# A two-layer gated transformer on one core: the opening of layer 1 reordered

## The chip, the cores and the metric

One core of a Trainium2 chip runs the whole computation in one launch. The core has these engines: PE (TensorE, matrix products), DVE (VectorE), ACT (ScalarE), POOL (GpSimd) and SP, whose queue issues nearly all transfers between the chip's memory (DRAM) and the on-chip memory; POOL has a queue for transfers of its own. Every queue works strictly in the order in which the program put its instructions. The metric is the device time of one execution in microseconds (us), median of several runs.

## The reference, cut to what matters

Eight sequences (elements) x of 512 tokens by 256 channels pass through two layers, each an attention part and a feed-forward part (ffn), each part added through a gate. Cut to the order of the parts:

```python
x = x + tanh(g_xattn[0]) * L0_xattn(layernorm(x), ctx)     # self + cross attention, 16 heads of 16
x = x + tanh(g_ffn[0])   * L0_ffn(layernorm(x))            # 8-bit quantised, scales over ALL elements
x = x + tanh(g_xattn[1]) * L1_xattn(layernorm(x), ctx)     # two blocks a1, a2 with an mlp each
x = x + tanh(g_ffn[1])   * L1_ffn(layernorm(x))            # ternary weights, conv of width 3
```

Two things matter for what follows. The second matrix product of L0_ffn takes h = gelu(...) quantised by a scale and a zero point that come from the minimum and maximum of h over all eight elements: it can't begin before the last h is known. And block a2 of L1_xattn attends from x to the normalised context, whose keys and values don't depend on x at all:

```python
yn = ln(ee)                       # ee: the context, 512 tokens by 128 channels
k = einsum('btc,hcd->bhtd', yn, wk); v = einsum('btc,hcd->bhtd', yn, wv)   # "second" keys and values
```

In layer 1, x first goes through two normalisations in a row (that of the layer and ln1; the kernel makes them in one step), then one more inside block a1; then come queries, keys and values, 16 heads of 32, the scores and their exponentials, the weighted sum, and the mlp (li1, li2, gelu, li3).

## The kernel before, in words

**Stages.** `layer0_xattn` keeps all eight x on chip. In its sixth and seventh turn `load1` (line 1460) loads the projection weights of layer 1, folds gains and biases into them, and keeps them: those of block a2 other than wq lie in a pool (`w8`) that ends with layer 0. `ctx0` writes the normalised, transposed context of each element to DRAM (`cd`). `layer0_ffn` (line 1525) makes h of each element (`range0`), writes it to DRAM (`hd`) and takes its extrema (line 1621); beside that, `keys2` (line 1629) makes the second keys and values of each element from `cd` (eight projections of 128x128 by 128x512 each), writes them to `kd` and `vd`. After the last extremum, scales are computed (line 1546 on), all tiles of layer 0 are given up, and `layer1_xattn` (line 1661) begins.

**Opening of layer 1.** `first(b)` (line 1807) completes layer 0 for element b, in two halves of 256 tokens: load a half of h (tile `hF`, one buffer), quantise on ACT (line 1828), clamp and cast to `hq` on DVE (lines 1830 and 1832, one buffer), multiply by w2 (tile `fw`) on PE, add to x (`xF`, line 1839), store that half of x to `xd` (line 1802). `pre1(b, half)` (line 1882) then loads the half back (tile `xP`, line 1798), normalises it for the layer and ln1 in one step (`ln_timed`, lines 1843 to 1862: statistics on DVE, a power on POOL, a scaling on ACT or DVE), adds rows (lines 1912 and 1914), normalises it again for block a1, stores the residual to `rd` (line 1918), turns it on PE into `zT`, and makes the values. `pair1` makes queries and keys of a group of four heads, `steps1` has the scores (`ps_s`), the exponentials (tile `pt`, three buffers, `PTS`), and the weighted sums. `load_mlp` loads li1, li2 and li3 of block a1 (2.5 MB, line 1770), `mlp1` (line 1969) uses them.

**The planner.** The order of all instructions is written out by a planner when the program is built. `Pace` (line 744) keeps an estimated clock per engine and per tile; transfers are planned one behind the other on one wire at 280 bytes per ns. Work is cut into streams, which are generators that say at each `yield` what they need next. `weave_all` (line 1713) holds chains of streams: `few` (the `first` of the elements, `load_mlp`, and `last`, the ffn of layer 1, sorted by base), `pairs`, two of `mlps`, two of `pres`, `diag`, beside the attention steps. Only the head of a chain can go on. At each point it takes, among the candidates that could start within 0.3 us of PE's planned time, the one of lowest `base + share * done / total`, where done is PE work planned so far; attention step n of the k-th of 16 slots has k + n/16. If none can start, it takes the one that can start soonest. The slots run element 0 block a1, element 1 block a1, element 0 block a2, element 1 block a2, and so on in pairs of elements. Each engine then runs in exactly that order, whatever the real times are.

**Lines that the change touches.** The streams of the opening are made here:

```python
for k, b in zip((-1, 0, 1, 2, 3, 4, 7, 8), range(B)):
    few.append(Stream(self.first(b), 3.8, 0.8, k))
    if not b:
        few.append(Stream(self.load_mlp(), 1.0, 1.0, k))
```

Of the kernel before, what the change touches and what calls it, by code (L numbers as in the profile page):

```python
# [15 lines left out]
P = 128  # L16
# [10 lines left out]
NEG = -1.0e30  # L27
PTS = 3


# [901 lines left out]
class Fast(General):  # L932
# [8 lines left out]
    def setup(self, ctx, ctx0):  # L941
        super().setup(ctx, ctx0)
        nc, tc = self.nc, self.tc
        dram = ctx.enter_context(tc.tile_pool(name="dram", bufs=1, space=bass.MemoryType.DRAM))

        def scratch(name, shape, dtype=F32):
            return [dram.tile(shape, dtype, name=f"{name}{b}") for b in range(B)]


        self.xd = [scratch(f"xd{k}_", [P, NT * C]) for k in range(3)]  # L950

        self.rd = scratch("rd", [P, NT * C])
        self.hd = scratch("hd", [P, NF * T])
        self.cd = scratch("cd", [P, T])
        self.kd = scratch("kd", [P, 4 * T])
        self.vd = scratch("vd", [P, NT * 2 * C])
        self.fwd = {
            n: dram.tile([P, 2 * FF], BF16, name=f"q_{n}")
            for n in ("f0_w1", "f0_w2", "f1_w1", "f1_w2")
        }  # L960
        keep = self.keep2
        self.ones = keep.tile([P, 32], F32, name="ones")
        nc.vector.memset(self.ones, 1.0)

# [495 lines left out]
    def load1(self, blk):  # L1460
# [13 lines left out]
        for name, nch, ln in (("wq", 2, "lnx"), ("wk", nchy, "lny"), ("wv", nchy, "lny")):  # L1474
# [14 lines left out]
            else:  # L1489
                for g in range(4):  # L1490
                    for c in range(nch):
# [3 lines left out]
                        )  # L1495
                bias = home.tile([P, 4], F32, name=f"{pre}_{name}_b")
                s = 32.0 ** -0.5 if name == "wq" else 1.0
# [6 lines left out]
        self.w1s.append(w)  # L1504
        if blk:

            a, e = at["li1"]
# [17 lines left out]
    def layer0_ffn(self):  # L1525
        nc, tc, small = self.nc, self.tc, self.small
        with (
# [101 lines left out]
    def keys2(self, b):  # L1629

        nc, work, w = self.nc, self.work, self.w1s[1]
        cT = self.cTs.pop(0)
        if b + 2 < B:
# [7 lines left out]
        v = work.tile([P, NT, 2 * C], F32, tag="v2", name="v2")  # L1641
        for kt in range(NT):
            yield need(cT)
            ps = self.bank()
            self.mm(ps, cT[:, 0, kt * P : (kt + 1) * P], w["wv"][:, 0, :])
            self.copy_of(v[:, kt, :], ps)
        nc.sync.dma_start(self.vd[b], v.rearrange("p t c -> p (t c)"))

# [12 lines left out]
    def layer1_xattn(self):  # L1661
        nc, tc = self.nc, self.tc
        with (
# [143 lines left out]
    def first(self, b):  # L1807
# [4 lines left out]
        def load_h(half):  # L1812
            h = work.tile([P, NF, n], F32, tag="hF", name="hF")
            nc.sync.dma_start(
                h, self.hd[b].rearrange("p (f t) -> p f t", f=NF)[:, :, half * n : (half + 1) * n]
            )
            return h

        h = load_h(0)
        w2, = self.few_weights(0, ("w2",))  # L1820
        x = self.load_x(0, b, "xF")
        yield need(x, pe=False)
        nc.gpsimd.tensor_tensor(x, x, self.gb2.unsqueeze(1).to_broadcast([P, NT, C]), ALU.add)
        for half in range(2):
            if half:
                h = load_h(1)
            yield need(h, pe=False)
# [11 lines left out]
            nc.vector.scalar_tensor_tensor(x2, ps, self.sg, x2, ALU.mult, ALU.add)  # L1839
            self.store_x(1, b, x2, half)  # L1840
            self.given.add((1, b, half))

# [39 lines left out]
    def pre1(self, b, half):  # L1882
# [86 lines left out]
    def mlp1(self, b, blk, half):  # L1969
# [3 lines left out]
        pre = ("a1", "a2")[blk]  # L1973
        while self.both_in.get((b, blk), 0) < 2:
            yield WAIT
# [488 lines left out]
```

## Time and profile before

| | us |
|---|---|
| median of 3 runs | 2920.08 |
| lowest and highest | 2911.39, 2924.05 |
| the profiled execution | 2911.77 |
| its span, first to last instruction | 2910.0 |
| PE busy | 2551.4 (88%) |
| DVE busy | 1707.2 (59%) |
| ACT busy | 1496.4 (51%) |
| POOL busy | 628.6 (22%) |
| DRAM traffic | 116.32 MB read, 62.39 MB written |

The page of the profile gives busy time by engine, the span in 40 slices of 72.75 us (a digit is the busy share in tenths), the transfer queues, and the costliest groups of instructions by line. The other views are: a table of busy time by stretch, the timeline of one engine (start, length, engine, line, operation, tiles written and read, and in brackets how long the engine stood idle before and what ended it), and who waited for whom. SPq is SP's queue: the length of its entries is the issue, not the transfer. Layer 0's attention ends near 770 us, its ffn at 911.7, and the attention of layer 1 runs from 980.7.

### The profile page before, as it was taken

How to read it: one execution, taken by the hardware profiler on the slowest of the kernel's cores; microseconds unless marked ns; L12 is line 12 of the kernel's file. 1: busy time of each engine (PE TensorE's matmuls, PEld its weight loads, DVE VectorE, ACT ScalarE, POOL GpSimd, SP SyncE). 2: the span in 40 equal slices, each digit the busy share in tenths (PEclk: the TensorE clock that was granted, in tenths of full speed). 3: DMA queues.
4: the chain of work that ended last, by engine and by line, in shares of the span. 5: the costliest groups of instructions: out<-in, count | busy, mean ns of one | idle time of the engine just before them, and what ended most of it. 6: DMA issues, size and time to landing. Idle time of an engine off the chain costs nothing. (4 is left out here: it accounts for less than half of the span.)

```text
span 2910.0 us, 38485 instructions
## 1 busy us (share of the span) xinstructions
PE 2551.4 (88%) x15431; PEld 1234.3 (42%) x15436; DVE 1707.2 (59%) x2998; ACT 1496.4 (51%) x1852; POOL 628.6 (22%) x691
## 2 busy tenths in 40 slices
PE   5999999999774889999988898998898998898976
PEld 2333333333232335535554534455443555353454
DVE  2434443444375465574657786746878446778574
ACT  2666666656584445555435555444555444455531
POOL 2111121121100343330423202322312122321010
PEclk9999999999997899999999999999999999999987
DMA  3011110100165312222110212220120111021100
GB/s 107 8 41 48 48 40 31 41 15 12 66 280 207 126 63 72 70 91 73 70 51 26 77 48 73 87 98 1 48 90 26 48 43 38 26 94 34 44 15 16
DMA packets 77179, 181.27 MB, mean 62 GB/s; under 512 B 7488, under 2 KB 36544, under 8 KB 69184
## 3 DMA queue, kind: packets, MB, share of 16 engines
q1 hardware_dynamic: 74768, 176.05, 17.4%
q8 instruction: 123, 2.02, 0.3%
q0 software_dynamic: 640, 2.10, 0.3%
q10 hardware_dynamic: 1584, 0.58, 0.1%
q14 instruction: 64, 0.52, 0.1%
HBM read 116.32 MB, written 62.39 MB: 61 GB/s over the span
## 5 line engine op out<-in xcount | busy, mean ns | idle before, releaser
L2084 ACT ACTIVATE pt<-ps_s 128x1024 f32<-128x1024 f32 x512 | 496.0, 1020 | 385.9 <-PE ps_s L1012 327.1
L1012 PE MATMUL ps_s<-QT,KT 32*128 32x512 f32 (+3 forms) x4096 | 634.1, 613 | 59.8 <-DVE KT L1655 26.3
L1371 ACT ACTIVATE pt<-ps_s 128x1024 f32<-128x1024 f32 (+3 forms) x512 | 411.6, 861 | 203.4 <-PE ps_s L1012 197.6
L1012 PEld LDWEIGHTS ps_s<-QT,KT 32*128 32x128 f32 x4096 | 199.3, 186 | 415.9 <-issue 235.3
L1012 PE MATMUL ov<-pt,v 128*32 128x512 f32 (+3 forms) x2048 | 237.9, 535 | 12.9 <-POOL pt L1374 12.5
L1012 PE MATMUL ps<-x3T,li 128*128 128x256 f32 x1024 | 247.3, 395 | 0.2 <-ACT x3T L2001 0.2
L2088 POOL TENSOR_SCALAR_AFFINE_SELECT dg<-pt 128x512 f32<-128x512 f32 x128 | 114.6, 897 | 593.0 <-ACT pt L2084 593.0
L1012 PE MATMUL ps<-li,hD 128*128 128x256 f32 x1024 | 236.3, 384 | 5.3 <-ACT hD L2031 5.3
L1012 PE MATMUL ov<-pt,vt 128*32 128x512 f32 (+3 forms) x1792 | 201.2, 520 | 36.4 <-DVE oT L2133 26.4
L1012 PEld LDWEIGHTS ps<-x3T,li 128*128 128x128 f32 x1024 | 196.5, 197 | 56.4 <-issue 18.0
L1012 PEld LDWEIGHTS ps<-li,hD 128*128 128x128 f32 x1024 | 189.6, 190 | 64.1 <-issue 17.7
L1856 POOL TENSOR_SCALAR mv<-mv 128x2 f32<-128x2 f32 (+1 forms) x105 | 61.9, 589 | 688.7 <-DVE mv L1851 631.5
L1374 POOL TENSOR_SCALAR_AFFINE_SELECT pt<-pt 128x512 f32<-128x512 f32 x128 | 86.8, 678 | 476.0 <-ACT pt L1371 476.0
L2115 DVE TENSOR_TENSOR acc<-acc,pt 128x2048 f32<-128x2048 f32 x64 | 148.6, 2323 | 6.9 <-ACT pt L2084 6.4
L2113 DVE TENSOR_TENSOR acc<-pt 128x2048 f32<-128x2048 f32 x64 | 151.2, 2362 | 1.0 <-ACT pt L2084 1.0
L2199 DVE SCALAR_TENSOR_TENSOR hF<-hp,cols,hF 128x256 f32<-128x256 f32 x224 | 121.9, 544 | 33.9 <-ACT hF L2190 27.4
L1396 DVE STREAM_TRANSPOSE ot<-ov 128x512 f32<-128x512 f32 x64 | 45.8, 716 | 155.8 <-PE ov L1012 155.8
L1012 PE MATMUL ps<-zT,a_wq 128*128 128x512 f32 x256 | 127.9, 623 | 1.4 <-DVE x3T L2003 1.1
L1012 PE MATMUL ps<-li,oT 128*128 128x256 f32 x512 | 126.6, 390 | 2.8 <-DVE oT L2133 2.2
L1012 PE MATMUL ps<-fw,hq 128*128 128x256 bf16 x512 | 72.6, 304 | 62.6 <-DVE hq L1832 44.6
L1015 PE MATMUL ps<-ident,z 128*128 128x128 f32 x328 | 64.5, 318 | 70.9 <-DVE z L136 40.9
L1655 DVE TENSOR_SCALAR hD<-ps,cols 128x256 f32<-128x256 f32 x145 | 66.9, 481 | 98.2 <-PE ps L1012 72.5
(277 smaller groups left out, 3666.2 us busy)
## 6 DMA issues: line engine op xcount, KB each, us to landing
hd<-h SPq DMA_DIRECT2D x16, 1024.0 KB, 3.9
hF<-hd SPq DMA_DIRECT2D x16, 1024.0 KB, 6.3
li<-in_w_a_dram SPq DMA_DIRECT2D x16, 1024.0 KB, 5.1
fw<-q_f_w SPq DMA_DIRECT2D x22, 512.0 KB, 5.8
xF<-xd SPq DMA_DIRECT2D x22, 512.0 KB, 5.3
kd<-k SPq DMA_DIRECT2D x8, 1024.0 KB, 4.0
vd<-v SPq DMA_DIRECT2D x8, 1024.0 KB, 5.5
res<-rd SPq DMA_DIRECT2D x32, 256.0 KB, 2.8
```

The costliest lines, as they stand in the source:

```text
L1012: self.nc.tensor.matmul(out, lhsT, rhs, start=start, stop=stop, skip_group_check=True)
L1015: self.nc.tensor.transpose(out, in_, self.ident)
L1371: nc.scalar.activation(pt[:, 2 * jp : 2 * jp + 2, lo:], pss[jp][:, :, lo:], AF.Exp)
L1374: nc.gpsimd.affine_select(out=diag, in_=diag, compare_op=ALU.is_ge, fill=0.0, base=0, pattern=[[0, 4], [1, P]], channel_multiplier=-1,)
L1396: nc.vector.transpose(ot.rearrange("p b d -> p (b d)"), ov)
L1655: self.nc.vector.tensor_scalar(out, ps, bias, None, ALU.add)
L1856: nc.gpsimd.tensor_scalar(rstd, mv[:, :, 1], EPS, None, ALU.add)
L2084: nc.scalar.activation(pt[:, 2 * jp : 2 * jp + 2, :], pss[jp], AF.Exp)
L2088: nc.gpsimd.affine_select(out=dg, in_=pt[:, :, diag], compare_op=ALU.is_gt, fill=0.0, base=0, pattern=[[0, 4], [-1, P]], channel_multiplier=1,
L2113: nc.vector.tensor_tensor(st["acc"], st["pt"], pt, ALU.add)
L2115: nc.vector.tensor_tensor(st["acc"], st["acc"], pt, ALU.add)
L2199: nc.vector.scalar_tensor_tensor(a, hp[:, half + k : half + k + n], self.col("conv_w", 3 * f + k), a, ALU.mult, ALU.add)
```

## The change

Four things are done.

1. The second keys and values of elements 6 and 7 are no longer made in the ffn of layer 0 but by a new stream `keys2_rest` in layer 1, base -1, share 1 over 16 us of work. Since their weights lie in a pool that has ended by then, `load1` writes them to DRAM (`wd`, two stores of 256 KB on SP), and the new stream loads them and the two contexts through POOL's queue (four loads of 256 KB) into tiles whose buffers the mlp uses later (`xo`, `x3T`); the keys and values themselves go into `pt` buffers, and from there to `kd` and `vd`. `mlp1` waits until all are made (`keys_done`). The bias wk_b now lies in a pool that lasts.
2. `first(0)` loads both halves of h at its start, the second into a `pt` buffer.
3. x of element 0 stays on chip in `xF`: `pre1(0, half)` reads it there in place of loading `xP`; its last normalisation writes into an `xP` tile. The store to `xd` stays, since block a2 reads it later. `first(1)`, whose x goes into the same buffer, waits until both halves have been read (`x0_read`).
4. `load_mlp` comes after `first(1)` in its chain, not after `first(0)`.

```diff
+KEYS_FIRST = 6
...
+        self.wd = [dram.tile([P, 2 * C], F32, name=f"wd{i}") for i in range(2)]
...
-                bias = home.tile([P, 4], F32, name=f"{pre}_{name}_b")
+                bias = self.keep2.tile([P, 4], F32, name=f"{pre}_{name}_b")
...
         if blk:
+            for i, name in enumerate(("wk", "wv")):
+                nc.sync.dma_start(self.wd[i], w[name].rearrange("p c f -> p (c f)"))
...
-            streams.append(Stream(self.chain(*(self.keys2(b) for b in range(B))), 64.0, B))
+            streams.append(Stream(self.chain(*(self.keys2(b) for b in range(KEYS_FIRST))), 64.0, B))
...
+    def keys2_rest(self):
+
+        nc, work = self.nc, self.work
+        w = []
+        for i in range(2):
+            t = work.tile([P, 1, 2 * C], F32, tag=f"xo{i}", name="w2")
+            nc.gpsimd.dma_start(t[:, 0, :], self.wd[i])
+            w.append(t)
+        cTs = {}
+
+        def load(b):
+            if b < B:
+                cTs[b] = work.tile([P, 1, T], F32, tag=f"x3T{b % 2}", name="cT")
+                nc.gpsimd.dma_start(cTs[b][:, 0, :], self.cd[b])
+
+        load(KEYS_FIRST)
+        load(KEYS_FIRST + 1)
+        for b in range(KEYS_FIRST, B):
+            k = work.tile([P, 4, T], F32, tag="pt", name="k2", bufs=PTS)
+            yield from self.keys_of(b, cTs[b], w[0], k)
+            v = work.tile([P, NT, 2 * C], F32, tag="pt", name="v2", bufs=PTS)
+            yield from self.values_of(b, cTs.pop(b), w[1], v)
+            load(b + 2)
+        self.keys_done = True
+
+    def keys_of(self, b, cT, wk, k):
+        bias = self.w1s[1]["wk_b"]
         for g in range(4):
-            yield need(cT)
-            ps = self.proj(w["wk"], cT, g * P)
-            self.plus(k[:, g, :], ps, w["wk_b"][:, g : g + 1])
-        nc.sync.dma_start(self.kd[b], k.rearrange("p g t -> p (g t)"))
+            yield need(cT, wk)
+            ps = self.proj(wk, cT, g * P)
+            self.plus(k[:, g, :], ps, bias[:, g : g + 1])
+        self.nc.sync.dma_start(self.kd[b], k.rearrange("p g t -> p (g t)"))
...
-                if not b:
+                if b == 1:
                     few.append(Stream(self.load_mlp(), 1.0, 1.0, k))
...
+            self.keys_done, self.x0_read = False, 0
+            keys = [Stream(self.keys2_rest(), 8.0 * (B - KEYS_FIRST), 1.0, -1.0)]
             self.weave_all(
-                [self.steps1(b, blk) for b, blk in order], [few, pairs, *mlps, *pres, diag]
+                [self.steps1(b, blk) for b, blk in order], [few, pairs, *mlps, *pres, diag, keys]
             )
...
         def load_h(half):
-            h = work.tile([P, NF, n], F32, tag="hF", name="hF")
+            if b or not half:
+                h = work.tile([P, NF, n], F32, tag="hF", name="hF")
+            else:
+                h = work.tile([P, NF, n], F32, tag="pt", name="hF", bufs=PTS)
...
+        while b == 1 and self.x0_read < 2:
+            yield WAIT
         h = load_h(0)
         w2, = self.few_weights(0, ("w2",))
         x = self.load_x(0, b, "xF")
+        h2 = None if b else load_h(1)
...
-                h = load_h(1)
+                h = h2 or load_h(1)
...
             self.store_x(1, b, x2, half)
+            if not b:
+                self.x0 = x
...
-        x = self.load_x(1, b, f"xP{half}", half)
+        if b:
+            z = x = self.load_x(1, b, f"xP{half}", half)
+        else:
+            x = self.x0[:, 2 * half : 2 * half + 2, :]
+            z = work.tile([P, 2, C], F32, tag=f"xP{half}", name="xP")
         yield need(x, pe=False)
         res = work.tile([P, 2, C], F32, tag=f"resP{half}", name="resP")
         yield from self.ln_timed(x, res, f"p{half}", of_ln=True)
-        yield from self.enter1(b, half, "ln1", "a1", res, x, f"p{half}")
+        self.x0_read += not b
+        yield from self.enter1(b, half, "ln1", "a1", res, z, f"p{half}")
...
-        while self.both_in.get((b, blk), 0) < 2:
+        while self.both_in.get((b, blk), 0) < 2 or not self.keys_done:
             yield WAIT
```

The new function `values_of` is the second half of the former `keys2`, with the weights given as an argument, as `keys_of` is the first.

More of the change, by code (lines that the diff above doesn't have):

```diff
@@ L1629, in keys2 @@
     def keys2(self, b):
-        nc, work, w = self.nc, self.work, self.w1s[1]
+        work, w = self.work, self.w1s[1]
         cT = self.cTs.pop(0)
-        if b + 2 < B:
+        if b + 2 < KEYS_FIRST:
             self.load_cT(b + 2)
         k = work.tile([P, 4, T], F32, tag="k2", name="k2")
-        for g in range(4):
-            yield need(cT)
-            ps = self.proj(w["wk"], cT, g * P)
-            self.plus(k[:, g, :], ps, w["wk_b"][:, g : g + 1])
-        nc.sync.dma_start(self.kd[b], k.rearrange("p g t -> p (g t)"))
@@ L1641, in keys2 @@
-        v = work.tile([P, NT, 2 * C], F32, tag="v2", name="v2")
+        yield from self.keys_of(b, cT, w["wk"], k)
+        v = work.tile([P, NT, 2 * C], F32, tag="v2", name="v2")
+        yield from self.values_of(b, cT, w["wv"], v)
+    def keys2_rest(self):
[19 more added lines that the diff above has]
+        self.keys_done = True
@@ L1642, in keys2, with values_of @@
+    def keys_of(self, b, cT, wk, k):
+        bias = self.w1s[1]["wk_b"]
+        for g in range(4):
+            yield need(cT, wk)
+            ps = self.proj(wk, cT, g * P)
+            self.plus(k[:, g, :], ps, bias[:, g : g + 1])
+        self.nc.sync.dma_start(self.kd[b], k.rearrange("p g t -> p (g t)"))
+    def values_of(self, b, cT, wv, v):
         for kt in range(NT):
-            yield need(cT)
+            yield need(cT, wv)
             ps = self.bank()
-            self.mm(ps, cT[:, 0, kt * P : (kt + 1) * P], w["wv"][:, 0, :])
+            self.mm(ps, cT[:, 0, kt * P : (kt + 1) * P], wv[:, 0, :])
@@ L1646, in keys2 @@
             self.copy_of(v[:, kt, :], ps)
-        nc.sync.dma_start(self.vd[b], v.rearrange("p t c -> p (t c)"))
+        self.nc.sync.dma_start(self.vd[b], v.rearrange("p t c -> p (t c)"))
     def plus(self, out, ps, bias):
```

## The prediction

> **What bounds the kernel now.** I read the page first, for where TensorE (PE) is not busy; then the table of busy time by stretch around that place; then the timeline of every engine there, step by step; last the waits of SP, whose queue feeds nearly all loads.
>
> ```profile
> span 2910.0 us, 38485 instructions
> ...
> PE   5999999999774889999988898998898998898976
> ...
> PEclk9999999999997899999999999999999999999987
> ```
>
> A slice is 72.75 us. PE is busy nearly everywhere except in slices 10 to 12 (727 to 946 us), where the granted clock falls too. That is the end of layer 0 and the opening of layer 1. Columns below: stretch, its length, busy time of PE, weight loads, DVE, ACT, POOL, then clock, DMA share, GB/s.
>
> ```profile
> 912.00:924.00 12.00, 0.25 (x2) 0.22 (x3) 4.31 (x16) 2.09 (x1) 0.86 (x3) 0.50 0.49 176
> ...
> 928.00:939.00 11.00, 0.00 (x0) 0.00 (x0) 3.18 (x6) 2.09 (x1) 1.59 (x2) 0.59 0.45 143
> ...
> 944.00:956.00 12.00, 7.30 (x12) 2.95 (x12) 3.20 (x9) 1.09 (x2) 2.22 (x3) 0.72 0.93 323
> 956.00:971.00 15.00, 5.03 (x21) 3.01 (x21) 8.46 (x14) 4.75 (x6) 8.55 (x7) 0.66 0.29 109
> ...
> 981.00:1053.00 72.00, 63.05 (x484) 23.19 (x476) 44.34 (x53) 40.08 (x42) 28.59 (x28) 0.93 0.19 63
> 1053.00:1069.00 16.00, 12.22 (x32) 5.42 (x28) 10.75 (x22) 3.88 (x7) 4.51 (x5) 0.89 0.05 17
> ```
>
> No engine is full between 912 and 971: this stretch is one chain of small steps and round trips to memory. From the timelines of SP, ACT, DVE and PE (start, length, engine, line; in brackets the engine's idle time before and what ended it):
>
> ```profile
> 912.08 0.62 SPq L1814 DMA_DIRECT2D hF<-hd  x1
> ...
> 918.92 2.09 ACT L1828 ACTIVATE hF<-hF,magic,qh_rs 128x2048 f32<-128x2048 f32 x1 [13.33 <-DMA fw<-q_f_w]
> ...
> 927.09 0.75 DVE L1839 SCALAR_TENSOR_TENSOR xF<-ps,sg,xF 128x512 f32<-128x512 f32 x1 [3.44 <-PE ps L1012]
> ...
> 928.23 0.53 SPq L1814 DMA_DIRECT2D hF<-hd  x1
> ...
> 934.76 2.09 ACT L1828 ACTIVATE hF<-hF,magic,qh_rs 128x2048 f32<-128x2048 f32 x1 [13.75 <-DMA hF<-hd]
> ...
> 943.18 0.75 DVE L1839 SCALAR_TENSOR_TENSOR xF<-ps,sg,xF 128x512 f32<-128x512 f32 x1 [1.76 <-PE ps L1012]
> ...
> 946.37 0.33 SPq L1798 DMA_DIRECT2D xP<-xd  x1
> ...
> 952.85 18.14 SPq L1918 DMA_DIRECT2D rd<-resP  x2
> ...
> 955.90 0.42 DVE L1850 BATCH_NORM_STATS2 mv<-xP 128x6 f32<-128x256 f32 x1
> ...
> 970.28 0.59 ACT L1930 COPY zT<-ps 128x512 f32<-128x512 f32 x1 [0.99 <-PE ps L1015]
> ...
> 980.66 1.14 PE L1012 MATMUL ps_s<-QT,KT 32*128 32x512 f32 x8 [0.94 <-DVE KT L1655]
> ...
> 1069.32 1.14 PE L1012 MATMUL ps_s<-QT,KT 32*128 32x512 f32 x8 [0.78 <-ACT KT L1653]
> ```
>
> See: the second half of h is asked for only when the first is consumed (928.23); the finished x goes out and comes back as xP, arriving 12.0 us after 943.93 because 2.5 MB of mlp weights (issued 944.32) go ahead; scores of element 0 begin at 980.66, those of element 1 at 1069.32, after a thin stretch from 1053.
>
> **The change, part by part.** All against the profiled execution, 2911.77 us (span 2910.0), which is 8.3 below the median 2920.08 and at the low end of the runs shown.
>
> **Layer 0.** Two 256 KB stores join SP after the scaling of a_wk and a_wv (DVE, done 601.8 and 605.8). SP waits there; behind it is the li_b load, which moves from 541.15 to about 606.5 and with its 6.2 us lands at 612.7, just before its matmuls at 613.20; the next SP item, the cd store, comes at 613.03. Cost 0, at worst 2 if that cover slips.
>
> **The ffn of layer 0 loses 16 projections**: PE 16 x 0.86 = 13.8 us, ACT 8 x 0.69 + 8 x 0.59 = 10.2 us. But the loop there is set by DVE: four reductions 8.87, two xq evacuations 1.40, then a gap until ACT has four gelus; the starts of the reductions lie 14.23, 13.51, 13.47, 13.51, 13.47, 14.18, 13.51 apart. Keys fill gaps. The only turn without keys beside its start (807.06 to 821.29) is one of the long ones: PE had stood 9.75 us and its twelve matmuls took 4.86 instead of 2.96. So the last two turns should be 14.2 each: **+0.7** (ends: -5 if the gap closed and DVE's own 11.0 per turn ruled, +1.4).
>
> **Loads at once.** hF behind nothing took 928.23 to 934.76, 6.5; hF with 1 MB behind it in the queue took 912.08 to 918.92, 6.8. So what follows in SP's queue delays it little; with 1 MB of hF and 1 MB from POOL added I take 919.5 (ends: 918.9, and 924 if all 4.2 MB shared 401 GB/s equally). POOL's four issues at 0.54 to 0.98 end by 917; its next work, xF plus bias, began at 924.12: covered. The first half is then done at 919.5 + 8.9 = 928.4 (before: 927.84).
>
> The Trainium skill, page "DMA: Bandwidth & Descriptors", section "Queues, rings and completion order", says that every DMA engine takes turns between the queues that have work, packet by packet, so POOL's megabyte would halve hF's rate. That would cost about 2.6 us (estimate, 1 MB at the trace's 401 GB/s) and make the sum -15 in place of -17.5; no stretch of this trace has both queues loaded at once.
>
> **Second half.** Its data lie there by about 924; only the cast waits, since hq has one buffer, read by PE until 927.6. But the planner decides PE's order: the keys stream has base -1 and rises 1 per 16 us of planned work, first(0) stands at -1 + 0.8 x 0.5 = -0.6 after its first half. So about 6.4 us of keys, seven projections at the planned 0.97, go ahead of first(0)'s second matmuls if their data are planned to be there, and by the planner's wire they are some 2 us earlier. Cost: two projections cold 3.75 (row at 775.17) and five at 0.86 = 8.05, so 935.7; matmuls 1.92 (warm row at 1010.16); evacuation 0.75: x complete at 938.4 against 943.93. Ends: 934 with no key ahead, 946 with all sixteen.
>
> **x kept on chip.** The trip 943.93 to 955.90 goes. The LN of the second half starts at 938.4, **17.5 earlier**. The rest of the chain, 955.90 to 980.66, is 24.8 long; nine key projections fall beside it, with 5.8 us of evacuations over ACT and DVE: +2 (0 to 2.9 each engine); PE no longer quite cold: transposes 1.39 and values 5.37 had 0.66 and 3.96 as warm rows, -1 of the possible 2.1. Scores begin **16.5 earlier**, at 964.
>
> **Shared buffers.** The second hF and the four key tiles take five turns of the three pt buffers, ahead of the scores' exponentials. The last key evacuation falls near 950, its store lands 5.5 later (median of vd), at 956, before 964: covered by 8 us; without that cover the third exponential waits for the rest.
>
> **Element 1.** Its first() now waits for both reads of x0: 938.4 + 3.6 (first LN, 955.90 to 959.45) = 942, against loads at 946.74, and without 2.5 MB of weights in front, so data by 949 against 959. Its second half is paced by the planner (matmuls 29.5 after the scores began, data long there), so it moves with the scores: no loss. The mlp weights now go ahead of element 1's last xP; before, 2 MB (element 2's hF, fw, xF) did: 0.5 MB more, **+1.3**. In return element 2's opening comes later; its DVE casts (4.9) and POOL addition (3.3) stood between that LN's statistics (to 1024.8) and its POOL step (1032.63): **-3** of 7.8 (0 to -7.8). li1 is used at 1053.35 - 16 = 1037 and issued near 997: 5.1 to 8.5 us per load, covered by some 25; if not, mlp1 waits, not the scores.
>
> **After that** every instruction is placed anew by the planner. Two equal stretches, 1500 to 2000 and 2000 to 2500, have 50.5 and 52.2 us of idle PE; scaled to 1800 us such luck is some 6 us either way. I take 0.
>
> Sum: -16.5 + 0.7 + 1.3 - 3 = **-17.5**: 2894.3 on the profiled execution, 2902.6 on the median. I give the middle, 2898.
>
> **Rivals.**
> *Keys don't push in* (first(0)'s second matmuls go first): x complete at 934, scores 4.4 earlier still, -22: 2890 to 2898. For it: the planner's data times for both lie within 2 us. Against: the lower key base.
> *Element 1 sets the pace*: if its readiness follows its loads (942.5 against 946.7) and not the scores, only 4 are won: 2908 to 2916. For it: PE already thins out at 1053 to 1069 waiting for it. Against: its second half was paced 29.5 after the scores.
> *Element 1's loads stick in SP* (slower): SP is in order, and before, the rd store of element 0's second half held it 17.3 us. If the loads of first(1) fall behind that store, they go at 942.5 + 17.3 = 960, 13 later than before; 122.6 us from loads to scores then give +13 to +14 with the +0.7: 2926. It decides from an issue later than 946.7. Against: the flag that frees first(1) is set one LN before that store is written into the queue.
>
> **How the numbers follow.** Chances: forecast 0.55, keys not pushing in 0.12, element 1 pacing 0.15, sticking loads 0.18. The measurement tells about 0.5%, 14.6 us. The forecast's own range is 2886 to 2911, three quarters of it beyond that bound; so faster 0.42 + 0.12 + 0.02, same 0.13 + 0.13 + 0.02, slower 0.16. The range 2878 to 2924 leaves out the far ends of the first rival and half of the last.
>
> **What would show it.** Right: ACT's second hF step directly behind the first; no xP load for element 0; LN of the second half near 938; scores of element 0 near 964 and of element 1 near 1050; key projections between 927 and 950; ffn of layer 0 ending within 1.5 us of 911.7. Wrong: keys filling PE before first(0)'s second matmuls for 16 us; hF landing after 922; first(1)'s loads after 947; scores waiting for a pt buffer that a key store still holds; the lead lost by 1300 us.

## The result and the profile after

The changed kernel takes 2898.17 us (median of 8 runs, 2887.04 to 2903.01); the kernel before took 2920.62 in the same comparison. The ratio is 0.9914, with a 95% interval of 0.9893 to 0.9936: 19 to 31 us faster. Forecast were 2898 and a range of 2878 to 2924.

The profiled execution took 2888.37 us, 9.8 below the median of its runs, as that of before was 8.9 below its own. From the page of the changed kernel, the span and the 40 slices (72.2 us each):

```profile
span 2886.6 us, 38491 instructions
...
PE   5999999999874989999988989998898998888976
...
PEclk9999999999987999999999999999999999999987
```

The hole is still there, in slices 11 to 13 (722 to 938 us), nearly all of it layer 0's ffn. In the slice behind it, the fourteenth, PE has 9 where it had 8, and its clock 9 where it had 8; at this grain there is no more to see.

Starting times shift by some us between executions for a reason that lies ahead of everything the change touches: of two stores in the start of layer 0 that all fourteen profiled executions have, the first is issued between 48.8 and 53.0 us, the next between 154.7 and 163.5, and the rest of layer 0 carries these 9 us along. So I count from one event, E, the last reduction that closes layer 0's ffn: 911.73 before, 916.74 after. The steps of the prediction in the timelines after:

```profile
917.10 0.62 SPq L1855 DMA_DIRECT2D hF<-hd  x1
...
918.92 1.09 SPq L1855 DMA_DIRECT2D hF<-hd  x1
...
923.62 2.09 ACT L1872 ACTIVATE hF<-hF,magic,qh_rs 128x2048 f32<-128x2048 f32 x1 [13.03 <-DMA hF<-hd]
...
930.83 2.34 POOL L1867 TENSOR_TENSOR xF<-xF,gb 128x1024 f32<-128x1024 f32 x1 [10.26 <-issue]
...
931.89 2.09 ACT L1872 ACTIVATE hF<-hF,magic,qh_rs 128x2048 f32<-128x2048 f32 x1 [6.18 <-DMA hF<-hd]
933.21 0.75 DVE L1883 SCALAR_TENSOR_TENSOR xF<-ps,sg,xF 128x512 f32<-128x512 f32 x1 [4.85 <-POOL xF L1867]
...
938.49 1.09 ACT L1908 ACTIVATE resP<-xF,mv 128x256 f32<-128x256 f32 x2 [4.50 <-DVE mv L1906]
939.49 1.24 ACT L1689 ACTIVATE k<-ps,a_wk_b 128x512 f32<-128x512 f32 x2
940.20 1.13 PE L1014 MATMUL ps<-cT,w 128*128 128x512 f32 x2 [4.32 <-ACT k L1689]
941.17 4.43 PE L1014 MATMUL ps<-w,cT 128*128 128x512 f32 x6
945.44 1.91 PE L1014 MATMUL ps<-fw,hq 128*128 128x256 bf16 x16
...
947.39 0.75 DVE L1883 SCALAR_TENSOR_TENSOR xF<-ps,sg,xF 128x512 f32<-128x512 f32 x1 [1.36 <-PE ps L1014]
948.17 0.43 DVE L1896 BATCH_NORM_STATS2 mv<-xF 128x6 f32<-128x256 f32 x1
948.53 0.53 SPq L1855 DMA_DIRECT2D hF<-hd  x1
...
956.94 0.73 DVE L137 TENSOR_SCALAR xP<-resP,mv 128x256 f32<-128x256 f32 x2 [0.47 <-POOL mv L1903]
...
968.65 1.14 PE L1014 MATMUL ps_s<-QT,KT 32*128 32x512 f32 x8 [0.84 <-DVE KT L1691]
...
1053.52 1.14 PE L1014 MATMUL ps_s<-QT,KT 32*128 32x512 f32 x8 [0.78 <-ACT KT L1689]
```

Both hF are asked for together; the first arrives in 6.5 us, the second in 13. Projections of the moved keys and values stand ahead of the second half's matmuls (tiles cT and w). The LN starts 0.03 us after the x it reads is complete, without a trip to memory. From E:

| us from E | before | forecast | after |
|---|---|---|---|
| x of element 0 complete | 32.2 | 26.7 | 31.4 |
| LN of its second half | 44.2 | 26.7 | 31.4 |
| its scores | 68.9 | 52.4 | 51.9 |
| scores of element 1 | 157.6 | 139.4 | 136.8 |

The scores come when forecast, but not by the steps forecast: the LN is 4.7 late, and the way from it to the scores 5.3 shorter.

Where the time went shows best in TensorE's busy time in three stretches of 50 us from E (columns: stretch, its length, busy time of PE, weight loads, DVE, ACT, POOL, then clock, DMA share, GB/s). Before:

```profile
911.73:961.73 50.00, 14.13 (x44) 7.32 (x44) 15.81 (x43) 9.44 (x9) 10.43 (x13) 0.64 0.53 184
961.73:1011.73 50.00, 44.30 (x247) 18.48 (x248) 27.52 (x37) 22.96 (x26) 17.15 (x17) 0.87 0.16 53
1011.73:1061.73 50.00, 38.25 (x291) 14.27 (x289) 33.45 (x42) 23.39 (x25) 20.78 (x18) 0.88 0.27 90
```

After:

```profile
916.74:966.74 50.00, 32.60 (x92) 15.48 (x93) 25.03 (x58) 15.75 (x19) 18.41 (x21) 0.79 0.58 210
966.74:1016.74 50.00, 46.15 (x325) 18.13 (x327) 27.98 (x39) 26.76 (x30) 17.09 (x17) 1.00 0.49 174
1016.74:1066.74 50.00, 42.81 (x306) 20.03 (x308) 32.76 (x54) 26.76 (x30) 23.57 (x23) 1.00 0.15 49
```

Busy time times granted clock, summed, is 81 us of full-speed work before and 115 after. Of the 33.5 more, 13.8 are the sixteen key projections that used to be in layer 0 (0.86 each), so the kernel is 20 us further on, nearly the 22.4 by which the medians differ. I call this number the lead (an estimate, since the clock of a stretch is a mean), and take it from stretches of 10 us below: 20.0 at 150 us from E, 21.3 at 400, 21.2 at 600.

### The profile page after: what moved, and what is told of

The parts are those of the page before. It is cut to its first block, busy times and chain, and to the rows that moved or that the text cites. A ratio compares the mean times of both kernels' runs of the same rounds, so it can differ in the third digit from the quotient of the medians.

```text
span 2886.6 us, 38491 instructions
## 1 busy us (share of the span) xinstructions
PE 2543.5 (88%) x15436; PEld 1231.9 (43%) x15436; DVE 1710.4 (59%) x3008; ACT 1490.2 (52%) x1840; POOL 628.3 (22%) x693
## 3 DMA queue, kind: packets, MB, share of 16 engines
q1 hardware_dynamic: 74768, 176.05, 17.4%
## 5 line engine op out<-in xcount | busy, mean ns | idle before, releaser
L1014 PE MATMUL ps_s<-QT,KT 32*128 32x512 f32 (+3 forms) x4096 | 634.3, 613 | 58.1 <-DVE KT L1691 26.2
L1398 DVE STREAM_TRANSPOSE ot<-ov 128x512 f32<-128x512 f32 x64 | 45.8, 715 | 157.6 <-PE ov L1014 157.6
L1689 ACT ACTIVATE hD<-ps,cols 128x256 f32<-128x256 f32 x111 | 50.8, 472 | 137.1 <-PE ps L1014 69.9
```

What stands on the lines that cost most here:

```text
L1014: self.nc.tensor.matmul(out, lhsT, rhs, start=start, stop=stop, skip_group_check=True)
L1689: self.nc.scalar.activation(out, ps, AF.Identity, bias=bias)
```

## The experiments

All landmarks are in us from E in the profiled execution; the difference is that of the medians against the kernel before on the same chip.

| | LN, half 2 | scores 0 | scores 1 | lead at 150 | lead at 400 | difference | ratio, 95% |
|---|---|---|---|---|---|---|---|
| before | 44.2 | 68.9 | 157.6 | 0 | 0 | | |
| after | 31.4 | 51.9 | 136.8 | 20.0 | 21.3 | -22.4 | 0.9893 to 0.9936 |
| e1 keys back | 24.9 | 55.4 | 138.5 | 13.3 | 12.8 | -14.3 | 0.9936 to 0.9970 |
| e2 keys late | 25.7 | 47.6 | 151.4 | 8.0 | 7.2 | -3.5 | 0.9975 to 1.0005 |
| e3 second hF late | 35.0 | 56.7 | 141.5 | 15.7 | 16.9 | -23.9 | 0.9894 to 0.9927 |
| e4 x reloaded | 40.1 | 61.0 | 144.2 | 7.8 | 7.3 | -21.1 | 0.9907 to 0.9940 |
| e5 keys back, hold | 25.7 | 55.5 | 135.7 | 14.7 | -4.3 | +6.6 | 1.0010 to 1.0028 |
| e6 keys mid | 25.5 | 52.7 | 134.4 | 16.0 | -1.8 | +1.8 | 0.9989 to 1.0016 |
| e7 late, own buffers | 26.2 | 49.2 | 143.3 | 12.8 | 13.1 | -14.6 | 0.9938 to 0.9963 |
| e8 mlp weights back | 31.2 | 51.7 | 140.0 | 15.3 | 8.5 | -5.2 | 0.9973 to 0.9992 |
| e9 only the keys | 43.6 | 68.3 | 156.9 | -0.5 | -0.1 | -1.5 | 0.9980 to 0.9997 |
| e10 only late weights | 48.8 | 71.4 | 154.3 | -1.8 | -3.1 | -5.5 | 0.9969 to 0.9990 |
| e11 before, later order | 44.3 | 68.9 | 157.5 | -0.4 | -2.1 | -3.4 | 0.9981 to 0.9998 |
| e12 after, later order | 32.0 | 52.5 | 137.4 | 19.1 | 18.6 | -23.7 | 0.9907 to 0.9934 |

The lead at 400 us and the difference agree within 6 us in all but e3 (7), e10 (9) and e4 (14); the profiled executions of e3 and e4 lay 5.3 and 10.5 above their medians.

**e1: the keys in layer 0 again**

```diff
-KEYS_FIRST = 6
+KEYS_FIRST = 8
...
-            for i, name in enumerate(("wk", "wv")):
-                nc.sync.dma_start(self.wd[i], w[name].rearrange("p c f -> p (c f)"))
...
-            self.keys_done, self.x0_read = False, 0
-            keys = [Stream(self.keys2_rest(), 8.0 * (B - KEYS_FIRST), 1.0, -1.0)]
+            self.keys_done, self.x0_read = True, 0
+            keys = []
```

> Undone here: the move of two elements' second keys (all eight elements' keys are made in the ffn of layer 0 again, no weights are stored and reloaded for them); the other three parts of the change stay. Times are counted from the last extremum of layer 0's ffn, E (before 911.73, changed kernel 916.74). Theory: the keys' move wins nothing by itself, since the ffn's turns are set by DVE, and it costs time in the opening, where seven projections stand in PE's order ahead of element 0's second half (LN of that half at E + 31.4 in the changed kernel). So the last two turns of the ffn stay at 27.7 +- 0.7 together, the LN of the second half starts at E + 23 to 25, the chain behind it is a little longer than 20.5 because PE is colder (22 to 25), scores at E + 46 to 49 (51.9 in the changed kernel), and the whole is 2 to 8 us faster than the changed kernel: 2890 to 2896. Rival: the move is what pays, because it takes 13.8 us of PE and 10.2 us of ACT out of the ffn: then the last two turns get 3 or more longer and the whole is 2904 or more.

The last two turns of layer 0's ffn took 14.18 and 13.51, after 13.57 and 14.23: the keys cost nothing there, and the longer turns by which the rival reached its total are not seen. The LN came at 24.9, as the theory had it, but the scores only at 55.4, and the total, 2909.7, is where the rival had it, by another way. The chain from LN to scores is 30.5 us, after 20.5. In e1 (DVE, ACT, PE; start, length):

```profile
954.60 0.69 DVE L1953 TENSOR_TENSOR vt<-ps,a_wv_b 128x512 f32<-128x512 f32 x1 [3.62 <-PE ps L1014]
955.21 0.42 DVE L1894 BATCH_NORM_STATS2 mv<-resP 128x6 f32<-128x256 f32 x1
...
956.92 1.34 DVE L1872 TENSOR_SCALAR hF<-hF,qh_lo,qh_hi 128x2048 f32<-128x2048 f32 x1
958.29 1.23 DVE L1874 TENSOR_SCALAR hq<-hF 128x2048 bf16<-128x2048 f32 x1
959.58 1.92 PE L1014 MATMUL ps<-fw,hq 128*128 128x256 bf16 x16 [3.30 <-DVE hq L1874]
961.60 0.75 DVE L1881 SCALAR_TENSOR_TENSOR xF<-ps,sg,xF 128x512 f32<-128x512 f32 x1 [2.08 <-PE ps L1014]
962.27 0.15 DVE L1904 SCALAR_TENSOR_TENSOR mv<-mv 128x2 f32<-128x2 f32 x1
962.52 1.09 ACT L1906 ACTIVATE xP<-resP,mv 128x256 f32<-128x256 f32 x2 [9.75 <-DVE mv L1904]
```

Two things stand on element 0's chain. Its second statistics wait in DVE's queue behind an evacuation of values that a slow TensorE delivers late (5.25 us for eight matmuls, after 3.70). And element 1's two casts, and the evacuation of its matmuls, stand in DVE's queue between those statistics and the normalization: 6.2 us from the end of the statistics (956.36) to 962.52. After, the same way takes 1.2 (955.74 to 956.94), because there the casts come behind it; before, it took 5.5, also with element 1's work beside it, but not by DVE's queue (see "The chain" below).

**e5: and element 1's first matmuls held back.** In e1 they stand ahead of element 0's last transposes.

```diff
+            while b == 1 and half == 0 and ("zT", 0) not in self.seqs[0]:
+                yield WAIT
             yield need(hq, x)
```

(The edits of e1 stand beside this one.)

> All sixteen key tiles are made in the ffn of layer 0 again, as in the run with the keys back, and the first matmuls of element 1's opening wait in the planner until both halves of element 0's z are turned. Counted from the last reduction of layer 0's ffn. Theory A (without keys to fill the gap the planner puts those matmuls, whose cast is late, between the values and the transposes of element 0's second half, and that costs the chain from LN to scores 8 to 10 of its 30.5 us): LN of the second half stays at 24 to 26, the chain shrinks to 20 to 24, scores of element 0 at 45 to 49, and the total falls from 2909.7 to 2897 to 2903. Theory B (the chain is long because TensorE has stood still and is cold, whatever the order): chain 28 to 31, scores 53 to 56, total 2906 to 2912. Theory C (element 1, not element 0's scores, sets the end): the chain shrinks as in A, but element 1's scores stay at 138 or come later, and the total stays at 2907 or more.

Theory A falls: the chain is 29.8 and scores of element 0 stay at 55.5. The casts are still in DVE's queue there, and eight values took 6.59 us at the low clock. B had that right, not the total. The total (2926.8) fell behind all others, which the opening does not explain: element 1's scores are 1.1 ahead of those after. The lead falls from 14.7 at 150 us to -4.3 at 400. Element 0's scores, the same as in e1, do not decide, as C has it, but the place is later still; C's own condition, a chain that shrinks, was not met.

**e2: the keys late; e7: late, in buffers of their own.** First diff e2, both diffs e7.

```diff
-            keys = [Stream(self.keys2_rest(), 8.0 * (B - KEYS_FIRST), 1.0, -1.0)]
+            keys = [Stream(self.keys2_rest(), 8.0 * (B - KEYS_FIRST), 1.0, -0.5)]
```

```diff
-            k = work.tile([P, 4, T], F32, tag="pt", name="k2", bufs=PTS)
+            k = work.tile([P, 4, T], F32, tag="hD0", name="k2")
...
-            v = work.tile([P, NT, 2 * C], F32, tag="pt", name="v2", bufs=PTS)
+            v = work.tile([P, NT, 2 * C], F32, tag="hD1", name="v2")
```

> One number is changed: the base of the stream of moved keys is -0.5 in place of -1, so that in PE's written order one key projection and not seven stands ahead of element 0's second half. Nothing else of the change is undone. Theory (PE's order holds the second half): the LN of that half starts at E + 23 to 25 in place of 31.4, scores at E + 44 to 47 in place of 51.9, the whole 4 to 8 us faster than the changed kernel, 2890 to 2894. Rival (the second half waits for its data or for DVE and ACT, not for PE's order): LN stays at E + 30 or later and the time stays within 2 us of the changed kernel.

> The late keys again (base -0.5), but with key tiles and value tiles in the two hidden-layer buffers, which are idle until the mlp starts, so that they hold none of the three buffers of the exponentials. Theory A (in the late-keys run element 1 was late because exponentials waited for buffers that key stores still held): the waits of ScalarE's exponentials for buffers, 17 us there, fall under 5, element 1's scores come at 136 to 142 from the last reduction against 151.4, total 2897 to 2905. Theory B (the projections and their evacuations among the scores cost it, whatever the buffer): element 1's scores at 146 to 152, total 2914 to 2921.

In e2 the LN comes at 25.7 and element 0's scores at 47.6, the earliest of all, nearly as the theory had it; yet the kernel is no faster than before. The moved projections now last until 1019 us, among the scores. Waits of ScalarE in e2 from 45 to 145 us after E (engine, tile and line, releaser: us in total, times, longest):

```profile
ACT pt L2135 <- DVE acc L2164: 10.7, 2, 6.3
...
ACT pt L2135 <- DVE acc L2166: 4.2, 1, 4.2
...
ACT pt L2135 <- DVE recs L2180: 2.5, 1, 2.5
```

Exponentials wait 17.4 us for a free pt buffer. With key tiles in the idle hidden-layer buffers none of these three waits is left in the same stretch of e7, element 1's scores come at 143.3 instead of 151.4, and the total falls from -3.5 to -14.6 against before. So the buffers cost 8 us of element 1 and about 11 of the total: theory A of e7, just outside its numbers (at most 142 and 2905; measured 143.3 and 2905.6). After, these waits come to 1.9 in that stretch.

**e6: the keys between element 0's second half and its scores**

```diff
-            keys = [Stream(self.keys2_rest(), 8.0 * (B - KEYS_FIRST), 1.0, -1.0)]
+            keys = [Stream(self.keys2_rest(), 8.0 * (B - KEYS_FIRST), 0.25, -0.55)]
```

> The changed kernel, with the two elements' keys given a base of -0.55 and a slope of 0.25 in place of -1 and 1: they no longer go ahead of the second half of element 0's ffn, but all sixteen still go ahead of the scores. Theory A (the keys cost only by standing ahead of that half; the harm of the late keys came from their lasting into the scores, where they hold the exponentials' buffers): LN of the second half at 24 to 27 from the last reduction, scores of element 0 at 47 to 51 against 51.9, no exponential waiting for a buffer, element 1's scores at 132 to 137, total 2892 to 2899. Theory B (the room is needed: keys put between LN and scores lengthen the chain by as much as they shorten the way to the LN): scores at 51 to 56, element 1's scores at 137 to 142, total 2898 to 2905.

The LN is 5.9 earlier than after, the scores 0.8 later: the keys put behind the LN cost 27.2 - 20.5 = 6.7 there, as B said. Element 1's scores are 2.4 earlier than after, as A said. The total is that of the kernel before, as neither said. TensorE's waits between 180 and 400 us after E, in e6:

```profile
PE ov L1014 <- DVE oT L2184: 12.7, 4, 5.4
PE ps_s L1014 <- DMA KT<-kd: 4.9, 2, 2.6
```

and after:

```profile
PE ov L1014 <- DVE oT L2184: 3.3, 3, 1.7
```

In that stretch TensorE stands 23.1 us in e6 as in e5, after 9.9, and the clock falls below 1.00 (0.66 in one stretch of 10 us), which it does not after. The planner has placed the work of the next attention steps differently. Which of its choices does it was not tried.

**e3 and e4: the second hF late, x reloaded**

```diff
...
-        h2 = None if b else load_h(1)
...
-                h = h2 or load_h(1)
+                h = load_h(1)
```

```diff
-        while b == 1 and self.x0_read < 2:
-            yield WAIT
...
-        if b:
-            z = x = self.load_x(1, b, f"xP{half}", half)
-        else:
-            x = self.x0[:, 2 * half : 2 * half + 2, :]
-            z = work.tile([P, 2, C], F32, tag=f"xP{half}", name="xP")
+        z = x = self.load_x(1, b, f"xP{half}", half)
```

> Undone here: the early load of element 0's second half of h; it is loaded into the same buffer after the first half again. All else of the change stays. Theory (the second half is on the chain that sets the opening): its load is issued near E + 17, lands near E + 24, its matmuls come behind ten keys and the first half's values, near E + 35; LN at E + 37 to 40, scores at E + 57 to 60, the whole 5 to 9 us slower than the changed kernel, 2903 to 2907. Rival (with seven keys ahead, the early load is hidden anyway): LN at E + 31 to 33 and no change beyond 2 us.

> Undone here: element 0's x kept on chip; each half is stored and loaded back for its LN again, and element 1's first part no longer waits for it. All else of the change stays, the mlp weights behind element 1 too. Theory: the trip is paid again, but without 2.5 MB of weights ahead of it it is a store of 2.3 and a load of 4 to 5 plus their issue, 7 to 8 and not the 12.0 of the kernel before; so LN of the second half near E + 38, scores near E + 59, the whole 5 to 8 us slower than the changed kernel, 2903 to 2906. Rival (element 1 sets the pace and was held by the wait for x0): scores of element 0 come later, those of element 1 stay at E + 137 +- 2 or come earlier, and the whole is not slower.

Element 0's scores come 4.8 and 9.1 later than after, element 1's 4.7 and 7.4: both parts do what they say in the trace, somewhat less than expected for hF (LN 35.0, expected 37 to 40). That the LN of e4 (40.1) comes near the expected 38 is luck: x is complete at 25.3, 6 us earlier than after, and the trip takes 14.8 instead of 7 to 8, of which 7.6 are the load behind element 1's loads and 4.7 a wait in DVE's queue, element 1's casts among what stands there. Why x is complete so early shows in the matmuls of e4 between the halves:

```profile
931.92 1.88 PE L1014 MATMUL ps<-cT,w 128*128 128x512 f32 x4
934.97 1.98 PE L1014 MATMUL ps<-cT,w 128*128 128x512 f32 x4 [1.17 <-DVE xF L1881]
...
939.97 1.91 PE L1014 MATMUL ps<-fw,hq 128*128 128x256 bf16 x16
```

The same seven projections stand ahead as after, but take 8.05 us instead of 13.6, because no LN scaling of element 0 is yet in ACT's queue ahead of their evacuations. In the clocked total neither e3 nor e4 can be told from the changed kernel: the 5 to 9 us that their theories expected did not come, and what these two parts win in the total is not shown.

**e8 and e10: the mlp weights ahead of element 1's loads again, and their move alone**

```diff
-                if b == 1:
+                if not b:
                     few.append(Stream(self.load_mlp(), 1.0, 1.0, k))
```

(e8, on the changed kernel; e10 is the opposite edit on the kernel before.)

> The changed kernel with the three mlp weights loaded right after element 0's opening again, ahead of element 1's loads. Theory A (the step of the prediction: element 1's second half is paced from element 0's scores, so its loads may be late, and 0.5 MB less stands ahead of its last xP): element 1's first half is 5 to 9 later, its scores at 134 to 138 from the last reduction against 136.8, total 2896 to 2900. Theory B (element 1's loads count): element 1's scores at 141 to 146, total 2903 to 2908.

> The last part of the change alone, in the kernel before: the three mlp weights are loaded after element 1's opening instead of after element 0's. Theory A (it gains only a few us at element 1, through its earlier loads and element 2's later opening): LN of element 0's second half at 43 to 48 from the last reduction, since 2 MB of element 1's loads take the place of 2.5 MB ahead of xP; element 1's scores at 151 to 158 against 157.6; total 2913 to 2921. Theory B (the place of these loads is worth some 15 us by itself, as the run with them put back lets one think): total 2900 to 2908.

Put back, they cost 3.2 us at element 1's scores, between A and B, and 17 of the total, more than either. Of the 17, the lead has 4.7 by 150 us and 8 more by 400. Element 1's first half is nearly as early as after (x complete at 57.3 against 56.7 from E), so it is not its loads. What differs is element 2: its hF is asked for 84.1 us after E instead of 86.1, and it goes through both halves by 127.5 instead of 199.9, so its casts, additions and LN run beside element 0's scores. TensorE's waits from 100 to 150 us after E for the tile that POOL makes of the exponentials, before, after and in e8:

```profile
PE ov L1012 <- POOL dg L2088: 7.3, 4, 2.9
```

```profile
PE ov L1014 <- POOL dg L2139: 2.1, 3, 1.0
```

```profile
PE ov L1014 <- POOL dg L2139: 4.0, 1, 4.0
```

These waits explain 1.9 us of the difference between e8 and after; what makes up the rest of the 17 was not tried. On the kernel before, the same move gains 5.5 us, within A (its LN, 48.8, is 0.8 beyond), and the lead at 400 us does not show even that (-3.1).

**e9: only the keys**

The edits of e3, e4 and e8 together, so that only the keys are moved.

> The first part of the change alone: the keys and values of two elements move into the opening of layer 1; the second hF, the reload of x and the mlp weights stay as before the change. Theory A (what wins the time is the shorter way to element 0's scores, and the keys alone don't shorten it): LN of the second half at 42 to 46 from the last reduction against 44.2 before, chain of 21 to 25 by the warmer TensorE, scores of element 0 at 64 to 70 against 68.9, total 2912 to 2922. Theory B (the keys win it by themselves, since they fill a TensorE that stands still 35.9 of the first 50 us): total 2900 to 2910.

A, to its numbers: LN 43.6, scores 68.3, -1.5 us. The chain stays at 24.7, although TensorE is busy for 26.8 of the first 50 us instead of 14.1.

**e11 and e12: another later order, the opening untouched**

```diff
-                    pairs.append(Stream(self.pair1(b, blk, g), 3.0, 0.2, k + 0.25 * (g - 1)))
+                    pairs.append(Stream(self.pair1(b, blk, g), 3.0, 0.2, k + 0.25 * (g - 1) - 0.1 * (k > 2)))
```

> The kernel before with one number of the planner changed, the place of the query and key projections from the fourth attention step on (0.1 of a step earlier); the opening of layer 1 keeps its order. Theory A (where the planner puts later work is worth some 6 us either way, as the prediction took it): total 2914 to 2926. Theory B (it is worth 10 to 20 us, so that part of any difference between two kernels here is such a draw): total below 2910 or above 2930.

> The changed kernel with the same number of the planner changed. Landmarks up to element 1's scores as in the changed kernel (element 0 at 51 to 53, element 1 at 136 to 138). Theory A (6 us either way): total 2892 to 2904, and 16 to 28 below the kernel before with the same number changed. Theory B: total above 2908 or below 2888, the difference to the other one anywhere between 0 and 40.

A for both: 2917.8 and 2897.5, 20.3 apart. The gain of the opening outlives this one different placement of the later work; e5 and e6 are placements that cost 18 to 19 us. No run beat the changed kernel by a difference that can be told.

## Why the prediction was right, point by point

**The total.** The sum was -17.5, and the medians differ by 22.4; up to element 1's scores the change wins 20.8, forecast 18.2. That 2898 is met to 0.2 is luck: it was the middle between the sum on the profiled execution (2894.3) and on the median (2902.6), and the second is 4.4 too high.

**Layer 0's stores at 0.** Right within 1 us: between two stores of layer 0 that all kernels have, near 430 and near 700 us, the changed kernel loses 0.7 (263.6 after 262.9), and e1, which has no such stores, nothing.

**The ffn turns at +0.7.** They cost 0.1: only the last of the two was long.

**"Loads at once".** First hF right: 6.5 us, no delay by POOL's loads. The second hF, planned for 924 with 4.2 MB at 401 GB/s as the worst case, was used only at 931.89, 15.2 after E and 2.9 beyond that case. The stretches of 3 us after:

```profile
920.00:923.00 3.00, 0.00 (x0) 0.00 (x0) 0.00 (x0) 0.00 (x0) 0.56 (x2) 0.50 1.01 355
923.00:926.00 3.00, 0.00 (x0) 0.00 (x0) 0.25 (x1) 2.09 (x1) 0.00 (x0) 0.50 1.02 397
926.00:929.00 3.00, 0.54 (x3) 0.43 (x4) 2.32 (x2) 0.00 (x0) 0.00 (x0) 0.50 1.02 365
```

The DMA engines are full for these 9 us (share 1.0). But the queue moved only 61, 216 and 273 GB/s in the three us from 918 to 921 and 209 in the last, from 930: the step was wrong in taking 401 GB/s, the rate from 916 to 919 in the kernel before, from start to end. The Trainium skill, page "DMA: Bandwidth & Descriptors", section "Queues, rings and completion order", has the engines take turns between queues: POOL's cT, issued from 919.50 and so behind SP's second hF, landed 9.0 us later and ahead of it, which agrees; the 2.6 on the first hF that the prediction worked out from this rule are not seen. They come on the second: without loads on POOL's queue (e1 and e5) it is used 12.9 after E, in the seven kernels that have them and ask for both hF at once 15.0 to 15.4. The prediction's remark that no stretch before has both queues loaded is wrong: POOL's cT of 822.67 took 5.6 us beside SP's stores, where the four from 771 to 794 have a median of 3.2.

**"Second half": seven keys ahead, 8.05 us.** They did go ahead, and put x back by 5.7 (in e2, with one key ahead, it is complete at 25.7) where the forecast with and without them differed by 4.4. The 4.7 by which x is late arise in TensorE's order, between the first key (931.83) and the second half's matmuls (945.44): 13.6 us instead of 8.05, from a start 0.8 earlier than forecast. TensorE stood 4.32 us of that time, for a bank that ACT was to empty while its queue held an LN scaling; the step had priced the projections and not their evacuations. In e4, without that scaling, they take the 8.05 forecast, and x is complete at 25.3. The late data of the second half are not what counts here: their cast is done at 937.66, 7.8 before the matmuls that read it.

**"x kept on chip": 17.5 earlier at the LN.** The trip went, as worked out; with x late it is 12.8.

**"The chain": 24.8, +2 for keys, -1 for the clock.** It measured 20.5. The step had missed that element 1's work stood inside that chain (5.5 us between statistics and normalization, of which 4.3 went), though it had used a like effect for element 1. In the kernel before, from the end of the statistics at 962.73 on:

```profile
962.89 1.15 POOL L1856 TENSOR_SCALAR mv<-mv 128x2 f32<-128x2 f32 x1 [1.37 <-DVE mv L1851]
964.12 1.65 POOL L1857 TENSOR_TENSOR mv<-mv,mhalf 128x2 f32<-128x2 f32 x1
965.75 2.34 POOL L1823 TENSOR_TENSOR xF<-xF,gb 128x1024 f32<-128x1024 f32 x1
...
965.81 2.30 DVE L1860 SCALAR_TENSOR_TENSOR mv<-mv 128x2 f32<-128x2 f32 x1 [0.59 <-POOL mv L1857]
```

DVE's queue holds nothing up here: its casts of element 1 end at 965.23, and it then stands 0.59 us for POOL. But POOL's two steps run beside those casts and take 1.15 and 1.65 us, against 0.22 and 0.70 after (from 955.90), and DVE's own step, 0.17 us at 958.16, takes 2.30 and ends with POOL's addition of element 1's x (968.11 and 968.09). e9 has the same four lengths to 0.01 us. In e1 it is DVE's order that holds the step. ScalarE's cast of element 1 starts 3.5 us after the LN in the kernel before (959.36), 6.9 after it in e1 (950.68) and 10.6 after it in the changed kernel (958.80), too late to get in between; in e1 the chain is 30.5. The warmer TensorE gave 2.2 (values 5.37 to 3.70, transposes 1.39 to 0.87), and projections of the moved values between the steps (964.21, 1.88) took 1.9 of it back. So the sum for element 0's scores, 16.5 against 17.0 measured, was right by two errors of 4.7 and 5.3 that cancel.

**"Shared buffers": covered by 8 us.** The cover was not there. The last moved value is evacuated at 971.57, 2.9 behind element 0's first scores, and its store, issued at 971.64, lands near 977 (estimate, by the 5.5 median of vd). It cost nothing that shows all the same: the third pair of exponentials, the first to need that buffer, starts at 978.34, when its scores are there. e2 shows what it costs when more keys come late.

**"Element 1": +1.3 and -3.** Together -1.7 forecast, -3.8 measured (its scores 84.9 behind element 0's, before 88.7). The mechanism was right, and larger than forecast: the 7.8 us between element 1's statistics and POOL's step are 0.3 after (1015.54 to 1015.81). e8 takes away the late element 2 and has 88.3; there element 2's casts stand ahead of those statistics, which come 101.2 after E instead of 97.6. The +1.3 was not measured by itself.

**"After that": 0, and 6 either way.** 0 was right for this kernel and for e12. The size is not: e5 and e6 lose 18 to 19 us of lead between 150 and 400 us, with element 1's scores even 1.1 and 2.4 earlier than here. A draw of that kind would have made the kernel no faster.

**The rivals.** Element 1 setting the pace was a better rival than its chance of 0.15: in e2 element 0 is 4.3 earlier than after, element 1 14.6 later, and the total 19 later by the differences of the table. It does not decide alone either: e5 and e6, the earliest at element 1, gain nothing. Its loads did not stick in SP (31.8 after E, ahead of the rd store at 42.3). That keys don't push in is e6's LN and e2's; forecast to gain 4.4 more, neither gained.

## What to carry over

Work that is moved to fill a standing engine also moves everything behind it in the queues of its helpers; read which other element's casts and additions stand inside the chain, in each engine's own order, and which small steps run beside them on another engine (POOL's step of 0.22 us took 1.15 beside DVE's casts), before its length is taken as given. Check a forecast made along one chain by a ledger of the bounding engine, busy time times granted clock over the stretch: here, read at 400 us, it gives the total within 6 us in ten of thirteen kernels, where the first landmark alone (element 0's scores) does not. Parts that look separate need not add up: two of the four gain 1.5 and 5.5 alone, yet taking them out of the whole costs 8 and 17.

## What the hardware showed

The granted clock counts for more than the forecast's 1 us. TensorE over stretches of 4 us (busy time, clock, DMA share, GB/s), before:

```profile
1023.73:1027.73 4.00, 2.40 (x16) 1.00 0.00 0
1027.73:1031.73 4.00, 2.92 (x16) 0.65 0.01 4
1031.73:1035.73 4.00, 3.13 (x24) 0.50 0.00 0
```

and after:

```profile
1020.74:1024.74 4.00, 3.00 (x28) 1.00 0.01 4
1024.74:1028.74 4.00, 2.38 (x25) 1.00 0.00 0
1028.74:1032.74 4.00, 3.62 (x42) 1.00 0.00 0
```

Before, the clock halves three more times beside the attention of element 0 (0.50 again in the 2 us from 1049.73 and from 1059.73). In the rows shown TensorE is busy 60 to 78% of the time, and its longest wait from 100 to 150 us after E is 2.9 us (for POOL). After, with waits up to 1.6, it stays at 1.00 from 30 us after E to 600. From 50 to 180 us the low clock takes 9.2 us of work before and none after, by busy time times what is missing to 1.00; in e1, where the keys are back in layer 0, it takes 6.6, and in e9, where only they are moved, 8.9. The Trainium skill, page "TensorE: Matmul & The Clock Gate", Part 1, has the clock fall after a window of about 3.4 us without work. For one kernel, the same Part of the Trainium skill's page has it swing because TensorE idles briefly but often between groups of matmuls. The first fall here came without such a window, as in that kernel, and 2.38 busy of 4 did not bring it down after the change. From which filling it falls stays open.
